# Two cross-attention layers in one kernel: layer 1's scores are computed once and kept in SBUF, and the row of maxima is added by VectorE and GpSimd

## The chip, the cores and the metric

The kernel runs on one core of one Trainium2 chip. The metric is the device time of one execution in microseconds (us); lower is better. Before the change the median of three runs is 3543.13 us (3540.61 to 3550.69). The engines are called PE (TensorE), DVE (VectorE), ACT (ScalarE), POOL (GpSimd) and SP (the queue that issues nearly all DMAs).

## The reference

Two layers of cross-attention follow each other, for 4 batches of 512 queries (320 channels, 20 heads of 16) over one context of 1024 tokens (512 channels), all in float32. In both layers the tokens fall into text and image ("ip") tokens with a softmax of their own. Cut to what matters:

```python
# layer 0: text = first 1020 tokens, ip = last 4
scores_t = einsum('bhsd,bhtd->bhst', q, k_t) * attn_scale
probs_t = softmax(scores_t)
text_out = einsum('bhst,bhtd->bhsd', probs_t, v_t)
attn_scores = einsum('bhsd,bhnd->bhsn', q, k_ip) * attn_scale
qsem = l2norm(einsum('bhst,bte->bhse', probs_t, text_ehs))
fused = attn_scores + 0.5 * einsum('bhse,bne->bhsn', qsem, l2norm(ip_ehs))
ip_out = einsum('bhsn,bhnd->bhsd', softmax(fused) * spatial_mask, v_ip)
x = (text_out + ip_out) @ W_out + b_out + x

# layer 1: text = first 77 tokens, ip = the other 947
out_text = attend(q, k, v, sm_scale)        # softmax over 77 tokens
out_ip = attend(q, k_ip, v_ip, sm_scale)    # softmax over 947 tokens
out = (out_text + out_ip) @ Wo.T + bo + x
```

Layer 1's queries come from layer 0's output; keys and values of both layers come from the context alone.

## The kernel before

A *turn* is 128 queries of one batch; there are 16 turns. A *group* is four heads of layer 0 in one turn, so there are 80 groups, and the main loop runs over them. Each group has two units (two heads each), each unit four parts (`part0` to `part3`, pieces of layer 0's large product of probabilities with values and context, tiles `b`), and after each part there is a *stop*, numbered k = 0 to 7 over the group. The function `stop` (L1054) puts other work between the parts:

- `item()`: one entry of a queue: the transposes of layer 1's maxima (`sub`), a turn's finishing steps (`late`), or a step of the next batch's projections (`proj`);
- at k = 0 and 1 `fill0`: one half (512 tokens) of layer 0's scores of the next group, `sc`, by 32 products in four row groups of PE; ACT copies them to SBUF (`e`), DVE reduces their maxima over the tokens that lie on one partition (`m`). The two score tiles are read by ACT and DVE in turn, and a tile's buffer is free when both are done;
- at k = 2 `max0`: PE transposes `m`, DVE reduces to one row (`zz`), transposes it (`zt`); SP writes it to DRAM (`zd`) and broadcasts it to all partitions (`bc`, 256 KB);
- at k = 4, 5, 5, 6 an entry of `ew` (end of `end_stop`): DVE adds the row to a quarter of the scores, ACT takes the exponential, POOL subtracts one half from the other for two of four;
- at k = 2, 4, 5, 6 `l1_step`: a step of layer 1, four to every four heads.

Layer 1 computes its scores twice. `do_max` multiplies queries by keys (`mx`, two products of 512 columns) with queries on the partitions and DVE reduces them from PSUM; `do_sub` transposes the negative maxima and adds them as extra rows to the queries (`qa`), next to rows of ones in `kq[1]` that choose between the text's maximum and the ip's. `do_exp` multiplies again (`ex`, 19 rows, two heads at a time) with tokens on the partitions, so that the maximum is already subtracted, and ACT takes the exponential straight from PSUM. `do_pv` multiplies by the values (`pv`), and `normalise` and `project` end the turn. After the last group the last turn's layer 1 runs alone (the tail).

PE, DVE and SP's broadcasts keep the order of the program text (`keep_in_program_order`); the other instructions are placed on their engine by the framework when the program is built, and each engine runs its own in that fixed order. The DVE operations of helper `vec` carry line 87, PE products 77, PE transposes 92.

A unit's parts depend on each other: `part2` adds products to a tile that DVE first has to copy (`p`, in `part1`), and `part3` adds to a tile that DVE first has to read (`c`, at the end of `part2`).

Of the kernel before, what the change touches and what calls it, by code (L numbers as in the profile page):

```python
# [20 lines left out]
P = 128  # L21
# [3 lines left out]
NIP = 4  # L25
# [30 lines left out]
def xattn_pair(ctx_stack: ExitStack, tc: tile.TileContext, a: dict, out: bass.AP):  # L56
# [9 lines left out]
    e1p = pool("e1p", 6)  # L66
# [61 lines left out]
    kq = [[cst.tile([P, T], F32, name=f"kq{l}_{i}") for i in range(1 + l)] for l in range(2)]  # L128
    qq = [[cst.tile([P, P], F32, name=f"qq{l}_{i}") for i in range(1 + l)] for l in range(2)]
    nmz = [cst.tile([P, P], F32, name=f"nmz_{i}") for i in range(2)]  # L130
    zz = cst.tile([P, ZW], F32, name="zz")
# [4 lines left out]
    own = cst.tile([H * NIP, H, D], F32, name="own")  # L136
# [59 lines left out]
    nc.vector.memset(zz, 0.0)  # L196
    nc.gpsimd.memset(wo1, 0.0)

    for i in range(2):
        nc.vector.memset(qq[1][i], 0.0)  # L200
        nc.vector.memset(nmz[i], 0.0)
# [7 lines left out]
    nc.gpsimd.tensor_copy(kq[1][1], kq[1][0])  # L209
# [7 lines left out]
    for n in ("21", "t4"):  # L217
# [10 lines left out]
                            pattern=[[-NIP, H], [0, D]], channel_multiplier=1)  # L228
    nc.gpsimd.affine_select(out=own, in_=own, compare_op=ALU.is_ge, fill=0.0, base=NIP - 1,
                            pattern=[[NIP, H], [0, D]], channel_multiplier=-1)  # L230
# [4 lines left out]
    def normalised_ip():  # L235
        ipraw = st2.tile([B * NIP, E], F32, tag="pc", name="ipraw")
        for b in range(B):
            nc.scalar.dma_start(ipraw[b * NIP : (b + 1) * NIP, :], a["ctx_2048"][b, NTXT0:T, :])
        ipsq = st2.tile([B * NIP, E], F32, tag="pc", name="ipsq")
# [63 lines left out]
    def queries(t, ns, w, dst, name, tag):  # L303

        n = ns * P
        o = st2.tile([P, NC, n], F32, tag=tag, name=f"qs_{name}")
# [18 lines left out]
    def projections(b):  # L325
# [11 lines left out]
        def quarter(n):  # L337
# [108 lines left out]
            def values_ip():  # L446

                w = load_w(b, "L0_xattn_W_v_ip")
                z.vip = st2.tile([H * NIP, C], F32, tag="vip", name=f"vip_{b}")
                rep = big.tile([P, EC, H, NIP], F32, tag="xin", name=f"iprep_{b}")  # L450
                nc.gpsimd.tensor_copy(rep, box["cT"][:, :, QT - NIP : QT].unsqueeze(2).to_broadcast([P, EC, H, NIP]))
                pt = tp(f"pt_vip_{b}")
                for e in range(EC):
                    mm(pt[: H * NIP, 0:C], rep[:, e].rearrange("p h n -> p (h n)"), w[:, e, 0:C], e == 0, e == EC - 1)
                vec.tensor_tensor(z.vip, pt[: H * NIP, 0:C], own.rearrange("p h d -> p (h d)"), ALU.mult)
# [33 lines left out]
    hold = [0]  # L489
    ready = {}  # L490
# [4 lines left out]
    def load_quad(l, z, turn, g):  # L495
# [3 lines left out]
        k = buffer(l, turn, g)  # L499
# [5 lines left out]
    def buffer(l, turn, g):  # L505
        return (turn * HG + g) % 2 if l else 0

    def fill(c, m, name):


        ps = [ps_sc.tile([P, 2, 512], F32, tag="sc", name=f"sc{name}_{c}_{i}") for i in range(2)]
        for j in range(TH):
            t = (TH * c + j) * P
            for r in range(4):
                mm(ps[r // 2][:, r % 2, j * P : (j + 1) * P], kq[0][0][32 * r : 32 * r + D, t : t + P],
                   qq[0][0][32 * r : 32 * r + D, :], True, True)
        e = [ep.tile([P, 2, TH, P], F32, tag="e0", name=f"e{name}_{c}_{i}") for i in range(2)]

        for i in range(2):
# [3 lines left out]
                              ps[j][:, :, 0 : (TH - c) * P].rearrange("p h (t s) -> p h s t", s=P), AX.X, ALU.max)  # L523
        return e

    def layer1(turn):

        b, s = TURNS[turn]  # L530
        z = zs[b]
        e1, ms, qas, vq, box = {}, {}, {}, {}, {}

        def name_of(g):
            return f"1_{turn}_{g}"

        def do_max(g, i, half):

            if g not in ms:
                ms[g] = st2.tile([P, 2, 4], F32, tag="m1", name=f"m{name_of(g)}")  # L540
            k, m = buffer(1, turn, g), ms[g][:, :, 2 * i : 2 * i + 2]
            if tail[0]:
                ps = [tail_bank(f"mx{name_of(g)}_{i}_{half}_{j}").unsqueeze(1) for j in range(2)]
            else:
                ps = [ps_sc.tile([P, 2, 512], F32, tag="sc", name=f"mx{name_of(g)}_{i}_{half}")]
            for j in range(2):
                r = 32 * (2 * i + j)
                o = ps[j][:, 0, :] if tail[0] else ps[0][:, j, :]
                mm(o, qq[1][k][r : r + D, :], kq[1][k][r : r + D, half * 512 : half * 512 + 512], True, True)

            def rows(row):
                return nmz[k].rearrange("p (r n) -> p r n", r=4)[:, 2 * i : 2 * i + 2, row]

            n = 2 // len(ps)
            for j, p in enumerate(ps):
                mine = slice(j * n, j * n + n)
                if half == 0:
                    vec.tensor_reduce(rows(R_TXT)[:, mine], p[:, :, 0:NTXT1], AX.X, ALU.max, negate=True)
                vec.tensor_reduce(m[:, half, mine], p[:, :, 0 if half else NTXT1 : 512], AX.X, ALU.max, negate=True)
            if half:  # L560
                vec.tensor_tensor(rows(R_IP), m[:, 0, :], m[:, 1, :], ALU.min)

        def do_sub(g):

            k = buffer(1, turn, g)
            pt = (tail_bank if tail[0] else tp)(f"pt_nm{name_of(g)}")
            tr(pt[:, 0:P], nmz[k], ident)
            qas[g] = st2.tile([P, P], F32, tag="qa", name=f"qa{name_of(g)}")
            vec.tensor_tensor(qas[g], pt[:, 0:P], qq[1][k], ALU.add)

        def do_exp(g, i, half):

            k, name = buffer(1, turn, g), f"{name_of(g)}_{i}_{half}"
            ps = ps_sc.tile([P, 2, 512], F32, tag="sc", name=f"ex{name}")
            for j in range(TH):
                t = (TH * half + j) * P
                for h in range(2):
                    r = 32 * (2 * i + h)
                    mm(ps[:, h, j * P : (j + 1) * P], kq[1][k][r : r + KR, t : t + P], qas[g][r : r + KR, :], True, True)
            e = e1p.tile([P, 2, TH, P], F32, tag="e1", name=f"e{name}")  # L580
            nc.scalar.activation(e.rearrange("p i j s -> p (i j s)"), ps.rearrange("p i n -> p (i n)"), AF.Exp)  # L581
            e1[g, i, half] = e

        def do_pv(g):

            v, name = vq.pop(g), name_of(g)
            e = [[e1.pop((g, i, half)) for i in range(2)] for half in range(2)]
            pv = tp(f"pv{name}")
            for r in range(4):
                mm(pv[32 * r : 32 * r + 32, P : 2 * P], v[:, 0, r * V1W : r * V1W + 32], e[0][r // 2][:, r % 2, 0, :],  # L590
                   True, True)
            for t in range(TT):
                for r in range(4):
                    mm(pv[32 * r : 32 * r + 32, 0:P], v[:, t + 1, r * V1W : r * V1W + 32],
                       e[t // TH][r // 2][:, r % 2, t % TH, :], t == 0, t == TT - 1)
            pc = st2.tile([P, 2 * P], F32, tag="pc", name=f"pc{name}")
            nc.scalar.copy(pc, pv[:, 0 : 2 * P])
            late.append(lambda: normalise(g, pc))

        def normalise(g, pc):  # L600
            if "o" not in box:
                box["o"] = big.tile([P, HG, P], F32, tag="o1", name=f"o1_{turn}")
            name = name_of(g)
            d = big.tile([P, 2 * P], F32, tag="den", name=f"den{name}")
# [25 lines left out]
        def values(g):  # L630
            if g < HG:
                vq[g] = st2.tile([P, TT + 1, V1Q], F32, tag="v1q", name=f"v1q_{turn}_{g}")
                nc.sync.dma_start(vq[g], z.v1d[:, :, g * 4 * V1W : g * 4 * V1W + V1Q])

        def load(g):
            load_quad(1, z, turn, g)

        def first_maxima(half):
            x = (turn * HG) % 2
            if half == 0:  # L640
                load(1)
                values(0)
            do_max(0, x, half)
            do_max(0, 1 - x, half)
# [3 lines left out]
        def step(g, k):  # L648


            x, half = (k + turn * HG + g) % 2, k // 2

            def after(n):

                return (me, g + n) if g + n < HG else (ready[turn + 1], g + n - HG) if turn + 1 in ready else None

            nxt = after(1)

            def maxima():
                if nxt and (g + 1 < HG or nxt[0].linked):  # L660
                    nxt[0].do_max(nxt[1], 1 - x, half)

            if tail[0]:

                if k == 0:
                    maxima()
                    if pend:
                        pend.pop()()
                if sub:
                    sub.popleft()()  # L670
                do_exp(g, x, half)
                if k:
                    maxima()
            else:
                maxima()
                if sub:
                    sub.popleft()()
                do_exp(g, x, half)
                if k == 0 and pend:
                    pend.pop()()  # L680
            if k == 1 and nxt and (g + 1 < HG or nxt[0].linked):
                nxt[0].values(nxt[1])
            if k == 3:
                pend.append(lambda: do_pv(g))
                if nxt and (g + 1 < HG or nxt[0].linked):
                    sub.append(lambda: nxt[0].do_sub(nxt[1]))
                two = after(2)
# [445 lines left out]
```

## Time and profile before

| | before |
|---|---|
| median of three runs | 3543.13 us |
| span of the profiled execution | 3537.1 us |
| first group to last group's start | 91.5 to 3364.2 us |
| `b` products on `xv_t`, mean of one record | 400 ns, 2560 records |
| ACT exponential of layer 1 from PSUM, 128x1024 | 1018 ns, 320 times |
| ACT copy of layer 0's scores, 128x1024 | 1012 ns, 320 times |
| DVE reduce of scores 128x1024 / 128x768 | 1220 / 957 ns, 160 times each |
| DVE add of the row, 128x1024 / 128x768 | 1227 / 995 ns, 160 times each |
| POOL operation on 128x512 with two SBUF inputs | 1269 to 1309 ns |
| broadcast `bc`, 256 KB | 80 times |

The page gives for each engine its busy time and share of the span, then slices of the span in tenths, then the chain of work that ended last. In a timeline a line is: start, time, engine, line, operation, tile written <- tiles read, shapes, count, and in brackets the idle time before it and what ended it. A product of PE appears as two records, and the ends of PE's records are modelled, so neighbours overlap: the time that a piece takes is read from its start to the next piece's start.

### The profile page before, as it was taken

The page shows a single profiled execution, that of the slowest core. Times are in us where ns is not written, and L with a number is a line of the kernel's source. Part 1 is how long each engine was busy: PE and PEld are TensorE (multiplying, and loading weights), DVE is VectorE, ACT ScalarE, POOL GpSimd, SP SyncE. Part 2 cuts the span into 40 slices and gives each one's busy share as a digit, 9 for nine tenths or more (in the row PEclk, how much of TensorE's full clock was granted, in tenths as well). Part 3 has the DMA queues.
Part 4 walks back from the last instruction along what each step waited for, and adds up shares of the span by engine and source line. Part 5 has one row for each costly group of instructions (what it writes and reads, how often), then busy time and mean ns, then how long its engine had stood idle before and what let it go on. Part 6 is the DMA issues. An engine that isn't in the chain of part 4 may idle for free.

```text
span 3537.1 us, 74110 instructions
## 1 busy us (share of the span) xinstructions
PE 3458.4 (98%) x29060; PEld 2757.2 (78%) x29060; DVE 2057.4 (58%) x3814; ACT 1477.9 (42%) x2807; POOL 993.7 (28%) x1050
## 2 busy tenths in 40 slices
PE   7999999999999999999999999999999999999989
PEld 6777777777787878777778888877778877777866
DVE  2344556666655655566665554656666666666644
ACT  1333344444434444444444443444444444444422
POOL 2322222332222222233222222222332332232310
PEclk9999999999999999999999999999999999999976
DMA  7454332222344244222234434322232222222211
GB/s 218 102 136 118 90 73 41 49 41 51 90 99 106 61 107 102 51 60 44 49 88 116 101 79 99 69 57 47 47 88 48 51 43 52 47 47 45 48 29 35
DMA packets 700570, 258.76 MB, mean 73 GB/s; under 512 B 567952, under 2 KB 673904, under 8 KB 700224
## 3 DMA queue, kind: packets, MB, share of 16 engines
q1 hardware_dynamic: 699184, 250.42, 31.5%
q8 instruction: 232, 3.80, 0.5%
q0 software_dynamic: 864, 3.41, 0.4%
q14 instruction: 114, 0.93, 0.1%
q10 hardware_dynamic: 176, 0.20, 0.0%
HBM read 213.51 MB, written 40.33 MB: 72 GB/s over the span
## 4 chain that ended last, share of the span: by engine, by line
PE 83%; DVE 9%; DMA 3%; issue 2%; SPq 2%; ACT 1%; POOL 0%; DVEq 0%; POOLq 0%; ACTq 0%
PE b L77 51%; PE ex L77 5%; PE sc L77 4%; PE pv L77 4%; PE pt_v L77 4%; PE mx L77 4%; PE pt_k L77 4%; DVE m L87 2%; PE pt_y L77 2%; DVE e L87 2%; PE pt_q L77 2%; DMA bc<-zd 2%; PE mx L92 1%; DVE den L87 1%; DVE n L87 1%
## 5 line engine op out<-in xcount | busy, mean ns | idle before, releaser
L77 PE MATMUL b<-xv_t,e 128*128 128x277 f32 x2560 | 659.6, 400 | 10.5 <-DVE c L87 9.9
L77 PE MATMUL b<-xv,e 128*128 128x277 f32 (+1 forms) x2560 | 651.2, 407 | 2.8 <-ACT e L778 2.8
L77 PEld LDWEIGHTS b<-xv,e 128*128 128x128 f32 x2560 | 479.7, 190 | 136.4 <-ACT e L778 3.3
L77 PEld LDWEIGHTS b<-xv_t,e 128*128 128x128 f32 x2560 | 473.0, 190 | 117.4 <-DVE c L87 15.9
L778 ACT ACTIVATE e<-e 128x1024 f32<-128x1024 f32 x320 | 338.2, 1057 | 407.6 <-DVE e L87 401.7
L873 POOL TENSOR_TENSOR e<-e,s 128x512 f32<-128x512 f32 x160 | 203.1, 1269 | 1028.0 <-PE b L77 1027.9
L87 DVE TENSOR_REDUCE m<-sc 128x256 f32<-128x1024 f32 (+1 forms) x320 | 341.6, 1089 | 160.9 <-PE sc L77 154.3
L87 DVE TENSOR_REDUCE m<-mx 128x2 f32<-128x870 f32 (+3 forms) x345 | 366.6, 1066 | 97.6 <-PE ex L77 74.3
L581 ACT ACTIVATE e<-ex 128x1024 f32<-128x1024 f32 x320 | 325.3, 1018 | 194.5 <-PE ex L77 194.2
L520 ACT COPY e<-sc 128x1024 f32<-128x1024 f32 x320 | 322.8, 1012 | 175.0 <-PE sc L77 131.6
L858 ACT ACTIVATE junk<-c 128x256 f32<-128x256 f32 x480 | 198.9, 414 | 460.5 <-DVE c L87 455.3
L87 DVE TENSOR_TENSOR e<-e,bc 128x1024 f32<-128x1024 f32 x320 | 355.2, 1111 | 59.4 <-DMA bc<-zd 59.1
L87 DVE TENSOR_TENSOR c<-b,p 128x256 f32<-128x256 f32 x320 | 133.6, 417 | 427.8 <-PE b L77 419.6
L77 PE MATMUL ex<-qa,kq 19*128 19x128 f32 x5120 | 377.0, 288 | 4.3 <-DVE qa L87 3.1
L77 PE MATMUL mx<-kq,qq 16*128 16x512 f32 x1280 | 375.8, 662 | 5.2 <-DMA qq<-q1d 2.9
L854 POOL TENSOR_TENSOR s<-e,e 128x512 f32<-128x512 f32 x160 | 203.6, 1273 | 472.6 <-ACT e L778 303.4
L77 PEld LDWEIGHTS ex<-qa,kq 19*128 19x128 f32 x5120 | 318.4, 191 | 16.8 <-issue 5.8
L77 PE MATMUL b<-xs,e 128*128 128x256 f32 x1280 | 319.7, 393 | 3.8 <-DVE p L87 3.3
L77 PE MATMUL b<-xs_t,e 128*128 128x256 f32 x1280 | 318.4, 392 | 1.3 <-POOL e L873 1.3
L780 POOL TENSOR_TENSOR e<-e 128x512 f32<-128x512 f32 x160 | 209.4, 1309 | 380.8 <-ACT e L778 380.8
L77 PE MATMUL b<-xs_t,s 128*128 128x256 f32 x1280 | 303.0, 379 | 0.4
L77 PEld LDWEIGHTS b<-xs_t,e 128*128 128x128 f32 x1280 | 230.4, 189 | 51.5 <-issue 13.7
(190 smaller groups left out, 4140.1 us busy)
## 6 DMA issues: line engine op xcount, KB each, us to landing
kq<-kd SPq DMA_DIRECT2D x640, 64.0 KB
v1q<-v1d SPq DMA_DIRECT2D x80, 373.5 KB
bc<-zd SPq DMA_DIRECT2D x80, 256.0 KB
xv<-v0d SPq DMA_DIRECT2D x480, 42.0 KB
xv_t<-v0d SPq DMA_DIRECT2D x320, 42.0 KB
L_xattn_W_k<-in_L_xattn_W_k_dram SPq DMA_DIRECT2D x13, 640.0 KB
L_xattn_Wv_ip<-in_L_xattn_Wv_ip_dram SPq DMA_DIRECT2D x13, 640.0 KB
raw<-in_ctx_dram SPq DMA_DIRECT2D x32, 256.0 KB
```

The source lines that it names most:

```text
L77: tc.keep_in_program_order(nc.tensor.matmul(out, lhsT=lhsT, rhs=rhs, start=start, stop=stop, skip_group_check=on))
L87: return lambda *args, **kw: keep(getattr(self.engine, name)(*args, **kw))
L92: tc.keep_in_program_order(nc.tensor.transpose(out, in_, ident))
L520: nc.scalar.copy(e[i].rearrange("p h t s -> p (h t s)"), ps[i].rearrange("p h n -> p (h n)"))
L581: nc.scalar.activation(e.rearrange("p i j s -> p (i j s)"), ps.rearrange("p i n -> p (i n)"), AF.Exp)
L778: nc.scalar.activation(flat, flat, AF.Exp)
L780: nc.gpsimd.tensor_tensor(e[:, 1], e[:, 1], e[:, 0], ALU.subtract)
L854: nc.gpsimd.tensor_tensor(self.s2, self.e("21"), self.e("22"), ALU.add)
L858: nc.scalar.activation(junk, x, AF.Square, accum_out=self.w["ss"][:, self.h + r, k : k + 1])
L873: nc.gpsimd.tensor_tensor(self.e("11"), self.e("11"), self.s2, ALU.add)
```

## The change

For all turns but the last, layer 1's scores are computed once, with tokens on the partitions, by the same `fill` as layer 0's: 32 products a half, ACT copies to SBUF, DVE reduces and a maximum of the halves. `Once.maxima` transposes the first block of 128 tokens and the maxima of the rest (eight transposes), DVE makes two rows (text and ip), which go by DRAM to all partitions in three broadcasts (512 KB in all). `Once.do_exp` adds the row: for the first half of the tokens on DVE, with the first 128-token block apart, for the second half on POOL; ACT takes the exponential from SBUF. `once(k)` replaces `l1_step` in `stop`: half fills at k = 3 and 4, maxima at k = 7, adds and exponentials at k = 2, 3, 6, 7 of the next group, `pv` at k = 1 after that. The last turn keeps the old way (`twice`) in the tail; there must be no layer-1 work left when it starts.

The buffer of keys for layer 1 is now single, the pool of `e` tiles for layer 1 has 8 buffers instead of 6, and tiles are moved between pools. Layer 0's scores of the four ip tokens are no longer kept from the transposes (`ips`): `load_ip_scores` loads queries and keys again and `exps` multiplies them in three products a turn. `values_ip` masks with two selections on POOL instead of a product with `own`.

```diff
-    e1p = pool("e1p", 6)
+    e1p = pool("e1p", 8)
...
-    kq = [[cst.tile([P, T], F32, name=f"kq{l}_{i}") for i in range(1 + l)] for l in range(2)]
+    kq = [[cst.tile([P, T], F32, name=f"kq{l}")] for l in range(2)]
...
-    def fill(c, m, name):
+    def fill(l, c, m, pl, tag, name):
...
+        lo, hi = (1 - c, TH) if l else (0, TH - c)
         for i in range(2):
             nc.scalar.copy(e[i].rearrange("p h t s -> p (h t s)"), ps[i].rearrange("p h n -> p (h n)"))
             j = 1 - i
             vec.tensor_reduce(m[:, c, 2 * j : 2 * j + 2, :],
-                              ps[j][:, :, 0 : (TH - c) * P].rearrange("p h (t s) -> p h s t", s=P), AX.X, ALU.max)
+                              ps[j][:, :, lo * P : hi * P].rearrange("p h (t s) -> p h s t", s=P), AX.X, ALU.max)
+        if c:
+            vec.tensor_tensor(m[:, 0], m[:, 0], m[:, 1], ALU.max)
         return e
...
+    class Once:
+
+        def __init__(self, turn, g, z, done, pl=None, tag="e1"):
+            self.turn, self.g, self.z, self.done, self.name = turn, g, z, done, f"1_{turn}_{g}"
+            self.pl, self.tag, self.e = pl or e1p, tag, {}
+            self.work = deque(lambda c=c, i=i: self.do_exp(c, i) for c in range(2) for i in range(2))
+
+        def fill(self, c):
+            if c == 0:
+                self.m = big.tile([P, 2, 4, P], F32, tag="m0", name=f"m{self.name}")
+            self.e[c] = fill(1, c, self.m, self.pl, self.tag, self.name)
+            if c:
+                loaded.clear()
+                load_next()
+
+        def maxima(self):
+
+            ps = ps_sc.tile([P, 2, 512], F32, tag="sc", name=f"mx{self.name}")
+            rest, first = [ps[:, k, :].rearrange("p (h t) -> p h t", h=4) for k in range(2)]
+            for h in range(4):
+                tr(first[:, h, :], self.e[0][h // 2][:, h % 2, 0, :], ident)
+            for h in range(4):
+                tr(rest[:, h, :], self.m[:, 0, h, :], ident)
+            z = zz[1]
+            vec.tensor_reduce(z[:, 0:4], first[:, :, 0:NTXT1], AX.X, ALU.max, negate=True)
+            vec.tensor_reduce(z[:, 8:12], first[:, :, NTXT1:], AX.X, ALU.max, negate=True)
+            vec.tensor_reduce(z[:, 4:8], rest, AX.X, ALU.max, negate=True)
+            vec.tensor_tensor(z[:, 4:8], z[:, 4:8], z[:, 8:12], ALU.min)
+            zt = st2.tile([P, ZW], F32, tag="zt", name=f"zt{self.name}")
+            vec.transpose(zt, z)
+            zd = spread(zt, 8, "zd1", self.name)
+            self.bc = bc = big.tile([P, 2, 4, P], F32, tag="bc1", name=f"bc{self.name}")
+            keep(nc.sync.dma_start(bc[:NTXT1, 0], zd[0:4, :].partition_broadcast(NTXT1)))
+            keep(nc.sync.dma_start(bc[NTXT1:, 0], zd[4:8, :].partition_broadcast(P - NTXT1)))
+            keep(nc.sync.dma_start(bc[:, 1], zd[4:8, :].partition_broadcast(P)))
+            self.v = load_values(self.z, self.turn, self.g)
+
+        def do_exp(self, c, i):
+            e, (first, rest) = self.e[c][i], [self.bc[:, k, 2 * i : 2 * i + 2, :] for k in range(2)]
+            if c == 0:
+                vec.tensor_tensor(e[:, :, 0, :], e[:, :, 0, :], first, ALU.add)
+            x = e[:, :, 1 - c :, :]
+            (nc.gpsimd if c else vec).tensor_tensor(x, x, rest.unsqueeze(2).to_broadcast([P, 2, TH - 1 + c, P]), ALU.add)
+            flat = e.rearrange("p h t s -> p (h t s)")
+            nc.scalar.activation(flat, flat, AF.Exp)
+
+        def values(self):
+            add_values(self.name, self.v, self.e, lambda pc: self.done(self.g, pc))
...
+    def load_next():
+        if waiting and not loaded:
+            turn, g, z, done = waiting[0]
+            load_quad(1, z, turn, g)
+            loaded.append(stops[0])
+
+    def take(*where):
+        if not loaded or stops[0] < loaded[0] + 2:
+            return None
+        o = Once(*waiting.popleft(), *where)
+        inside.append(o)
+        return o
...
         def exps():
+            pt = tp(f"pt_s_{name}")
+            for c, (c0, n) in enumerate(CK):
+                mm(pt[:, 0 : H * NIP], qf[:n, c, :], kip[:n, c].rearrange("p h n -> p (h n)"), c == 0, c == NC - 1)
             vec.tensor_tensor(sem, sem, wide(rn), ALU.mult)
-            vec.scalar_tensor_tensor(pe, sem, SEM_SCALE, ips, ALU.mult, ALU.add)
+            vec.scalar_tensor_tensor(pe, sem, SEM_SCALE, pt[:, 0 : H * NIP].rearrange("p (h n) -> p h n", h=H),
+                                     ALU.mult, ALU.add)
...
-        if k in (2, 4, 5) or k == 6 and gi < len(G) - 2 or ending[0] and k < 2:
-            l1_step()
         if k == 2:
             max0(gi + 1)
+        once(k)
         end_stop(k)
+
+    def once(k):
+
+        if k in ((0, 3) if ending[0] else (3,)):
+            filling[0] = take(*((ep, "e0") if ending[0] and k == 0 else ()))
+        o = filling[0]
+        if o and k in (0, 3):
+            o.fill(0)
+        if o and k in (1, 4):
+            o.fill(1)
+        if o and k in ((2, 7) if ending[0] else (7,)):
+            o.maxima()
+            o.ready = stops[0] + 3
+            filling[0] = None
+        if inside:
+            first = inside[0]
+            if not first.work and k == 1:
+                inside.popleft().values()
+            elif first is not filling[0] and k in (2, 3, 6, 7) and first.work and stops[0] >= first.ready:
+                first.work.popleft()()
```

## The prediction

> **What bounds the kernel now.** I read the page first (engine totals, clock, chain), then TensorE's waits, then the timeline of one group, then single waits. A group is one pass of the main loop: four heads of layer 0, eight stops k = 0 to 7, 80 groups in all.
>
> ```profile
> PE 3458.4 (98%) x29060; PEld 2757.2 (78%) x29060; DVE 2057.4 (58%) x3814; ACT 1477.9 (42%) x2807; POOL 993.7 (28%) x1050
> PEclk9999999999999999999999999999999999999976
> PE 83%; DVE 9%; DMA 3%; issue 2%; SPq 2%; ACT 1%; POOL 0%; DVEq 0%; POOLq 0%; ACTq 0%
> ```
>
> TensorE (PE) is busy in nearly every slice at its full clock until the tail (the last two digits); the other engines have room. The list of waits gives PE 9.9 us on VectorE's `c` and 3.3 us on its `p` in the whole span. So a group costs its PE work: the timeline has one without extra items from 3174.94 to 3210.96, 36.0 us. What a layer-1 piece costs must be read from starts, not from the groups' busy times, because two products overlap:
>
> ```profile
> 3178.91 1.17 PE L77 MATMUL sc<-qq,kq 16*128 16x128 f32 x32
> 3180.01 0.48 PE L77 MATMUL b<-xs_t,e 128*128 128x256 f32 x1
> ...
> 3202.99 0.70 PE L77 MATMUL mx<-kq,qq 16*128 16x512 f32 x2
> 3203.01 0.71 PE L77 MATMUL ex<-qa,kq 19*128 19x128 f32 x8
> 3203.53 0.59 PE L77 MATMUL mx<-kq,qq 16*128 16x512 f32 x2
> 3203.55 0.61 PE L77 MATMUL ex<-qa,kq 19*128 19x128 f32 x8
> 3204.10 0.48 PE L77 MATMUL b<-xs,e 128*128 128x256 f32 x1
> ```
>
> Both kinds of scores run side by side: one layer-1 step takes 3204.10 - 3202.99 = 1.1 us, although `mx` and `ex` show some 376 us of busy time each. Half a fill of layer 0 (`sc`) takes the same 1.1 us.
>
> **PE work.** Per four heads of layer 1 the change removes four steps (4.4) and the transpose of `nmz` (0.1). It adds two half fills (2.2) and eight transposes; four of them take 3190.16 - 3189.66 = 0.5, so 1.0. That is 1.3 us less in each of the 75 groups that carry layer 1: -97. New products for the IP scores, nine-product `pt_q` being 2.0 us: 3/9 of it, 0.65 x 16 = +10. Net -87.
>
> **What goes to the others.** VectorE loses per four heads the reduces on `mx` (2 x 1.22 + 2 x 1.05 + 2 x 0.31 + 2 x 0.22 = 5.6) and `qa` 0.3; it gains reduces 2 x 0.96 + 2 x 1.22, the maximum 0.69, three reduces on transposes, `zz`'s minimum and transpose (together 1.95), and adds 2 x (0.34 + 0.97): 9.6. ScalarE gains four copies of 1.01, GpSimd two adds. SP gains seven issues of 0.33 and 512 KB of broadcast; it and the DMA queues (31.5% busy) have room, and the single layer-1 `kq` is reloaded at k = 4 for k = 3 of the next group, over 20 us of cover for eight issues. Initial memsets, `own` and the dropped `ips` copy lie beside PE. The totals fit (VectorE some 28 of 35 us a group), but order matters: the built program's order on each engine is fixed, and three places make PE wait.
>
> **First wait: a broadcast, two GpSimd adds and ScalarE's queue.** On ScalarE the two exponentials fed by GpSimd stand, in nearly every group, ahead of the copies of layer 0's second half fill (k = 1). Behind those copies stand VectorE's second reduce, its maximum and both `drop` maxima; behind these PE's transposes at k = 2 and VectorE's two `c`, which PE's last product of the unit waits for. Let 0 be the start of the group's first product, the transposes of the row of maxima ending there (they are at k = 7). The row goes the same way as layer 0's:
>
> ```profile
> 3191.77 0.21 DVE L87 STREAM_TRANSPOSE zt<-zz 128x32 f32<-128x32 f32 x1
> 3192.01 1.25 SPq L765 DMA_DIRECT2D zd<-zt  x4
> 3195.22 0.34 SPq L767 DMA_DIRECT2D bc<-zd  x1
> 3198.93 1.23 DVE L87 TENSOR_TENSOR e<-e,bc 128x1024 f32<-128x1024 f32 x1 [0.30 <-DMA bc<-zd]
> ```
>
> VectorE ends `zt` at 1.5 (reduces of 308 and 204 elements run under the second four transposes, then 512 elements 0.69, minimum 0.2, transpose 0.2). Four `zd` issues: 2.8. In SP's order three `xv` windows follow, the last released by the product that ends at 4.0: 4.6. Three `bc` issues of 0.34: 5.65. Landing 3.4 after the issue's end (row above): 9.1. One GpSimd add of 1024 elements: the 512-element row takes 1.27 and the 256-element row 0.73, so 2.35. Adds end at 11.5 and 13.8; second exponential (1.06) at 15.0; copies at 16.0 and 17.0; reduce 17.0, maximum 17.7, two `drop` maxima 18.7; PE transposes at 18.8. PE itself is there after 4.0 + 1.1 + 3.65 + 1.1 + 2.1 (`pv`) + 3.8 = 15.75. With the two `c` (2 x 0.42) its next product starts at 19.65, not 16.25: **3.4 us**. If `bc` is issued as `zd` lands and all land together, 8.6 and 2.8 us; if 512 KB in three parts take turns, 10.7 and 5.0 us. I take 3.4, as the row's 256 KB are the nearest. Cover comes only from items at k = 0 to 2. Read from the starts of the groups in the timeline, some 21 of the 75 hold the next batch's projections (43 to 50 us each, the others 36.0 to 40.7) and are covered, since each of their stops brings PE work of its own; the query product (2.0) and small items (0.5) help in 11 groups each: 54 x 3.4 - 27 = **+157**.
>
> **Second and third wait: emptied stops.** The old steps at k = 5 and 6 stood between dependent products. After the second layer-1 fill (k = 4) VectorE has two reduces 2.44, maximum 0.69, layer 0's add 1.23, copy `p` 0.42 = 4.8, PE only 3.65 before it needs `p`: 1.0 to 1.6, taken as 1.4. At k = 6 PE waits for `c`; where no step stood there, before shows it:
>
> ```profile
> 3397.54 0.42 DVE L87 TENSOR_TENSOR c<-b,p 128x256 f32<-128x256 f32 x1 [1.37 <-PE b L77]
> ...
> 3398.02 2.13 PE L77 MATMUL b<-xv_t,e 128*128 128x277 f32 x8 [0.52 <-DVE c L87]
> ```
>
> 0.52 to 0.65. `multiply` and the next transposes cover both in 11 groups: 43 x (1.4 + 0.65) = **+88**.
>
> **The port.** GpSimd can hold up VectorE or be held up:
>
> ```profile
> 625.39 1.22 DVE L87 TENSOR_TENSOR e<-e,bc 128x1024 f32<-128x1024 f32 x1
> ...
> 625.37 2.38 POOL L780 TENSOR_TENSOR e<-e 128x512 f32<-128x512 f32 x1 [6.60 <-ACT e L778]
> ```
>
> GpSimd's 1.27 became 2.38, longer by VectorE's add. In the new window VectorE mostly reads PSUM; closer packed adds at k = 5 may collide: 0 to 1.3 a group, taken 0.5 x 54 = **+27**. The Trainium skill ("SBUF — State Buffer", Who interferes with whom) says a VectorE operation with two SBUF inputs and a GpSimd operation that reads SBUF exclude each other for the whole instruction, against handing adds to GpSimd; if that hit both new adds once a group by 1.2 us, the first wait would grow by up to 2.4.
>
> **The clock.** After a wait of 2.32 us by TensorE:
>
> ```profile
> 3402.70:3406.10 3.40, 1.16 (x6) 0.40 (x10) 2.70 (x9) 0.76 (x3) 0.00 (x0) 1.00 0.08 18
> 3406.10:3409.50 3.40, 3.40 (x68) 3.40 (x71) 1.84 (x7) 0.00 (x0) 0.00 (x0) 0.50 0.00 0
> ```
>
> the second stretch (the column after POOL is the granted clock) ran at 0.50, losing 1.7 us of work. At 3.4 us a wait this can come in most uncovered groups, partly under the second wait: 0 to +90, taken **+25**. The Trainium skill ("TensorE: Matmul & The Clock Gate", Part 1) puts the gate at a whole idle window of about 3.4 us; by that a 3.4 us wait would almost never close it and the term would be 0; the row closes it after 2.32.
>
> **The tail** keeps its old form; two `pv` replace steps beside the same late chain: -5 to +10, taken +5.
>
> Sum: -87 + 157 + 88 + 27 + 25 + 5 = +215 on the profiled 3537.1, 3752; the runs' median lies 6.0 above that span, so **3758**.
>
> **Rivals.**
> - *The rows hide the new waits* (faster). Only PE work changes: 3543 - 87 = 3456. It decides if `bc` lands so early that both adds and exponentials end before PE's half fill at 9.85, a landing near 3. For it: PE is 98% busy, all others under 60%. Against it: the `zd` and `bc` way alone takes 7 us above.
> - *Only the emptied stops cost*: -87 + 88, about 3544, the same, if the first wait is swallowed.
> - *Port and VectorE bind*: every GpSimd add blocks a two-input VectorE operation, 28 + 12 us, groups of over 42: 3543 + 54 x 6 = 3867 and above.
> - *The gate stays at half* as in the tail (the last slices' 7 and 6), groups far longer, 4000 or more.
>
> **How the numbers follow.** Forecast 0.70, its own range 3640 to 3890 (wait 2.8 to 5.0, clock 0 to 90, port 0 to 70); hidden 0.10; same 0.05; port 0.11; gate 0.04. 0.3%, 11 us, is what a measurement can tell. Faster 0.10, same 0.05, slower 0.85. The range 3530 to 3900 takes in the forecast's own and the case of no change; it leaves out the hidden case, the gate and the upper half of the port, some 0.19.
>
> **What would show it.** After: groups of about 40 to 42 us where they were 36.0; PE busy well under 98%; waits of PE's `mx` on `m` and of `b` on `p` and `c`; ScalarE idle on GpSimd's `e`; slices with PEclk under 9. If PE is still near 98% and ScalarE's wait for GpSimd ends before the copies, the prediction is wrong.

## The result, and the profile after

The changed kernel takes 4057.26 us (median of 4 runs, 4046.72 to 4069.05) beside 3546.91 us for the kernel before: 1.143 times as long, 95% interval 1.1398 to 1.1463. The forecast was 3758, with a range up to 3900. So the direction was right and the size too small by more than half: 215 us more were forecast, 510 came.

The page of the profile after, its lines that answer to those shown of before (engine totals, granted clock, chain by engine):

```profile
PE 3556.2 (88%) x28481; PEld 2773.4 (68%) x28481; DVE 2517.8 (62%) x4101; ACT 1758.1 (43%) x3107; POOL 1502.7 (37%) x1242
PEclk9999999999999999999999999989999999999986
PE 52%; DVE 15%; DMA 11%; POOL 8%; ACT 6%; issue 3%; SPq 3%; DVEq 0%; POOLq 0%; ACTq 0%
```

TensorE went from 98% to 88% busy, and its share of the chain from 83% to 52%: more of the time now goes the way from TensorE through the other engines and back. The profiled span grew by 525.0 us (3537.1 to 4062.1). TensorE's idle time grew by 427.2 (from 3537.1 - 3458.4 = 78.7 to 505.9), and its busy time grew too, by 97.8, although it has 579 instructions fewer. The clock digits are nines, which hides the second fact: a digit averages over some 100 us.

The waits of TensorE in the profile after (us in total, number, longest):

```profile
PE b L77 <- ACT u L935: 131.7, 54, 5.5
PE mx L92 <- DVE m L87: 87.6, 45, 3.2
PE b L77 <- DVE p L87: 87.2, 45, 3.4
PE b L77 <- DVE c L87: 45.6, 84, 1.1
PE pt_p L92 <- ACT pc L545: 29.1, 15, 4.6
PE mx L92 <- DVE pT L87: 23.9, 15, 2.0
```

One group in the timeline after, from TensorE's first product at 3550.78 (start, duration, engine, operation; in brackets the idle time before it and its releaser):

```profile
3550.78 4.04 PE L77 MATMUL b<-xv,e 128*128 128x298 f32 x16
...
3551.76 0.18 DVE L87 COPY pv<-b 128x21 f32<-128x21 f32 x1 [1.49 <-ACT junk L907]
3551.86 1.34 DVE L87 TENSOR_REDUCE zz<-mx 128x4 f32<-128x308 f32 x3
...
3553.03 1.27 POOL L922 TENSOR_TENSOR e<-e,s 128x512 f32<-128x512 f32 x1 [0.27 <-PE b L77]
3553.24 1.08 DVE L87 TENSOR_TENSOR zz<-zz 128x4 f32<-128x4 f32 x1
3554.36 0.21 DVE L87 STREAM_TRANSPOSE zt<-zz 128x32 f32<-128x32 f32 x1
...
3558.38 0.35 SPq L587 DMA_DIRECT2D bc<-zd  x1
...
3563.78 4.65 POOL L595 TENSOR_TENSOR e<-e,bc 128x1024 f32<-128x1024 f32 x2 [7.60 <-DMA bc<-zd]
...
3566.16 1.06 ACT L597 ACTIVATE e<-e 128x1024 f32<-128x1024 f32 x1 [7.87 <-POOL e L595]
3567.12 0.35 ACT L935 COPY u<-b 128x256 f32<-128x256 f32 x1
3567.53 2.13 PE L77 MATMUL b<-xv_t,e 128*128 128x277 f32 x8 [2.82 <-ACT u L935]
3568.47 1.06 ACT L597 ACTIVATE e<-e 128x1024 f32<-128x1024 f32 x1 [0.99 <-POOL e L595]
3569.43 1.91 ACT L519 COPY e<-sc 128x1024 f32<-128x1024 f32 x2
...
3572.81 1.09 PE L92 MATMUL mx<-ident,m 128*128 128x128 f32 x4 [3.15 <-DVE m L87]
```

Read it as one queue. ScalarE stands still for 7.87 us until GpSimd's first add ends; behind the exponential stands the copy `u`, which TensorE waits for (2.82); behind the second exponential stand layer 0's copies, behind these VectorE's maxima, and TensorE waits a second time (3.15). The four transposes then take 1.09 us; four took 0.5 before. The windows of the same stretch say why (stretch, busy us of PE, PEld, VectorE, ScalarE, GpSimd, then the granted clock, DMA share, GB/s):

```profile
3569.40:3572.80 3.40, 0.26 (x2) 0.02 (x1) 2.27 (x4) 2.21 (x4) 0.00 (x0) 0.99 0.49 96
3572.80:3576.20 3.40, 3.39 (x10) 2.51 (x11) 3.37 (x7) 1.02 (x4) 0.19 (x1) 0.51 0.12 29
```

After a stretch with 0.26 us of TensorE's work the next one runs at half clock. Such stretches come to 496.2 us in the profiled span after and to 117.4 in that of before. Before, most of that lies in the tail (95.5 us); after, 77 stretches lie in the main loop, 372 us in all, each one to three times 3.4 us long. At half clock half of the time is lost.

### The profile page after: what moved, and what is told of

Its sections match the earlier page's. It is cut to its first block, busy times and chain, and to the rows that moved or that the text cites. A ratio compares the mean times of both kernels' runs of the same rounds, so it can differ in the third digit from the quotient of the medians.

```text
span 4062.1 us, 74077 instructions
## 1 busy us (share of the span) xinstructions
PE 3556.2 (88%) x28481; PEld 2773.4 (68%) x28481; DVE 2517.8 (62%) x4101; ACT 1758.1 (43%) x3107; POOL 1502.7 (37%) x1242
## 4 chain that ended last, share of the span: by engine, by line
PE 52%; DVE 15%; DMA 11%; POOL 8%; ACT 6%; issue 3%; SPq 3%; DVEq 0%; POOLq 0%; ACTq 0%
PE b L77 32%; DMA bc<-zd 8%; POOL e L595 8%; DVE m L87 6%; DVE e L87 5%; PE sc L77 5%; PE pt_v L77 3%; ACT e L597 3%; PE pt_k L77 3%; PE mx L92 2%; ACT e L519 2%; PE pt_q L77 2%; PE pt_y L77 2%; PE pv L77 2%; DVE c L87 1%
## 5 line engine op out<-in xcount | busy, mean ns | idle before, releaser
L87 DVE TENSOR_REDUCE m<-sc 128x256 f32<-128x1024 f32 (+1 forms) x620 | 664.4, 1088 | 723.2 <-ACT e L519 440.1
L77 PE MATMUL b<-xv_t,e 128*128 128x277 f32 x2560 | 772.6, 451 | 178.5 <-ACT u L935 131.7
L519 ACT COPY e<-sc 128x1024 f32<-128x1024 f32 x620 | 610.9, 1010 | 169.6 <-PE sc L77 118.4
L87 DVE TENSOR_TENSOR e<-e,bc 128x1024 f32<-128x1024 f32 (+1 forms) x620 | 672.9, 1105 | 0.8 <-issue 0.4
L597 ACT ACTIVATE e<-e 128x1024 f32<-128x1024 f32 x300 | 316.8, 1056 | 690.7 <-POOL e L595 538.5
L595 POOL TENSOR_TENSOR e<-e,bc 128x1024 f32<-128x1024 f32 x150 | 351.3, 2362 | 482.4 <-DMA bc<-zd 482.4
L827 ACT ACTIVATE e<-e 128x1024 f32<-128x1024 f32 x320 | 338.3, 1057 | 343.1 <-DVE e L87 340.7
L77 PE MATMUL b<-xs,e 128*128 128x256 f32 x1280 | 326.5, 399 | 87.2 <-DVE p L87 87.2
L77 PEld LDWEIGHTS sc<-qq,kq 16*128 16x128 f32 x9920 | 313.4, 189 | 127.3 <-issue 107.1
L77 PE MATMUL sc<-qq,kq 16*128 16x128 f32 x9920 | 374.0, 286 | 13.5 <-ACT e L519 10.2
L829 POOL TENSOR_TENSOR e<-e 128x512 f32<-128x512 f32 x160 | 249.4, 1559 | 313.9 <-ACT e L827 309.2
L77 PEld LDWEIGHTS b<-xs,e 128*128 128x128 f32 x1280 | 240.6, 196 | 152.4 <-issue 119.2
L77 PEld LDWEIGHTS b<-xs_t,s 128*128 128x128 f32 x1280 | 243.8, 190 | 33.4
```

The costliest lines, as they stand in the source:

```text
L77: tc.keep_in_program_order(nc.tensor.matmul(out, lhsT=lhsT, rhs=rhs, start=start, stop=stop, skip_group_check=on))
L87: return lambda *args, **kw: keep(getattr(self.engine, name)(*args, **kw))
L519: nc.scalar.copy(e[i].rearrange("p h t s -> p (h t s)"), ps[i].rearrange("p h n -> p (h n)"))
L595: (nc.gpsimd if c else vec).tensor_tensor(x, x, rest.unsqueeze(2).to_broadcast([P, 2, TH - 1 + c, P]), ALU.add)
L597: nc.scalar.activation(flat, flat, AF.Exp)
L827: nc.scalar.activation(flat, flat, AF.Exp)
```

## The experiments

All times are medians; each ratio is to the kernel before, run on the same chip in the same job. e1, e2, e10 and e11 are edits of the changed kernel, e3 to e8 of e1, e9 and e12 of e7. The last two columns come from the profiled run of each; that of e4 took 3753.5 us and that of e7 3543.4, so they lie off the medians. Half clock is the time in the profiled span in which the granted clock was 0.5.

| run | us | ratio (95%) | PE busy us | half clock us |
|---|---|---|---|---|
| changed kernel | 4057.3 | 1.1430 (1.1398 to 1.1463) | 3556.2 | 496.2 |
| e1 exponentials in order | 3719.6 | 1.0487 (1.0455 to 1.0519) | 3432.2 | 226.4 |
| e2 adds on VectorE | 3689.0 | 1.0402 (1.0377 to 1.0427) | 3418.0 | 183.3 |
| e3 layer 0's adds later | 3670.1 | 1.0341 (1.0311 to 1.0370) | 3418.6 | 182.1 |
| e4 fill at k = 5 | 3733.3 | 1.0534 (1.0499 to 1.0569) | 3457.2 | 292.2 |
| e5 `p` on ScalarE | 3624.6 | 1.0209 (1.0182 to 1.0236) | 3391.0 | 151.2 |
| e6 maxima at k = 6 | 3660.6 | 1.0320 (1.0296 to 1.0344) | 3422.9 | 243.6 |
| e7 = e5 and e6 | 3556.3 | 1.0026 (1.0008 to 1.0044) | 3370.7 | 104.5 |
| e8 = e7, adds on VectorE | 3638.1 | 1.0255 (1.0233 to 1.0277) | 3434.3 | 230.1 |
| e9 = e7, three small waits | 3530.8 | 0.9953 (0.9938 to 0.9969) | 3381.9 | 122.9 |
| e10 changed kernel with filler | 4178.6 | 1.1780 (1.1762 to 1.1798) | 3952.8 | 186.0 |
| e11 needed row first | 3987.6 | 1.1237 (1.1217 to 1.1258) | 3536.1 | 431.5 |
| e12 `p` ahead of a copy | 3554.0 | 1.0021 (1.0006 to 1.0037) | 3402.8 | 182.3 |

**e1: only ScalarE's order.** The edit pins the two exponentials behind what ScalarE was given before them; nothing else is edited.

```diff
-            nc.scalar.activation(flat, flat, AF.Exp)
+            x = nc.scalar.activation(flat, flat, AF.Exp)
+            if c:
+                keep(x)
```

> Only the two exponentials of layer 1's second half (fed by GpSimd's adds) are pinned behind what ScalarE was given before them, so that on ScalarE they stand behind layer 0's copies at k = 1 instead of ahead of u and of these copies. Nothing is removed: the same 150 GpSimd adds, the same broadcast. Theory A (ScalarE's order is the first wait): TensorE's waits on u (131.7 us) and of mx on m (87.6) go nearly to nothing, and with them most of the half-clock stretches (TensorE's busy 3556 falls towards 3371 + 60): 4057 - 219 - 120 = about 3720, between 3640 and 3800. Theory B (the broadcast and GpSimd are late whatever the order, and TensorE then waits elsewhere for the same row): under 80 us gained, over 3975. Theory C (the gate, not the waits, is what costs: TensorE stays at half clock once per group for the waits on p and c that are left): waits go but busy stays at about 3550, 3830 to 3900.

Measured: 3719.6, as theory A put it. ScalarE in one group of e1's timeline: `u` and both copies run when their inputs are there, and the exponentials come at the end.

```profile
3271.01 0.37 ACT L937 COPY u<-b 128x256 f32<-128x256 f32 x1 [1.32 <-PE b L77]
3272.19 2.09 ACT L519 COPY e<-sc 128x1024 f32<-128x1024 f32 x2 [0.81 <-PE sc L77]
...
3283.34 1.06 ACT L597 ACTIVATE e<-e 128x1024 f32<-128x1024 f32 x1 [1.71 <-DVE e L87]
```

And TensorE's waits in e1:

```profile
PE b L77 <- DVE p L87: 122.0, 45, 3.4
PE b L77 <- DVE c L87: 49.6, 102, 1.1
PE mx L92 <- DVE pT L87: 18.9, 15, 2.8
PE mx L92 <- DVE m L87: 18.7, 18, 2.6
```

The wait on `u` fell from 131.7 to 0.2, on `m` from 87.6 to 18.7, on `pc` from 29.1 to 0.5, and waits of `pv` on ScalarE's evacuations (19.8) went: 249 us less idle. Busy time fell by 124 with the same instructions, and the wait on `p` rose by 35, since TensorE now comes to it earlier: 249 + 124 - 35 = 338 of the 346 us by which the span fell. Theories B and C fall. The broadcast, GpSimd's adds and their lateness are still there (the first add starts 11.8 us after the group's first product, 12.3 in the changed kernel; medians of groups 8 to 78), yet TensorE's waits on `u`, `m`, `pc` and of `pv` come to 19.4 us in place of 268. Two thirds of the loss was the place of two exponentials in one queue.

**e2: the second half's adds on VectorE.**

```diff
-            (nc.gpsimd if c else vec).tensor_tensor(x, x, rest..., ALU.add)
+            vec.tensor_tensor(x, x, rest..., ALU.add)
```

> Layer 1's second-half adds go to VectorE instead of GpSimd; as VectorE runs in program order, the exponentials behind them also come at k = 6 and 7, as in e1. Theory A: the first wait goes as in e1, and VectorE gets 150 x 1.22 = 183 us more, 2.4 of some 40 us a group, at k = 6 and 7 where c follows: e1's time plus 0 to 60. Theory D (sharing a port with GpSimd is what slows VectorE: the minimum of 128x4 took 1.08 us beside a GpSimd operation): VectorE's other rows get shorter (reduces, minimum) by more than it gains, GpSimd's rows go back to 1270 to 1310 ns, and this is faster than e1 by 20 us or more. Theory B: no gain over the changed kernel beyond 80 us.

Measured: 3689.0, 31 faster than e1, but not for theory D's reason. GpSimd's remaining operations did not get shorter: the subtraction of 128x512 elements at 1554 ns, 1475 in e1, 1309 before the change. VectorE's adds of 1024 elements stayed long too: 1573 ns, 1533 in e1, 1227 before. So the adds given to GpSimd are not what makes these rows longer; what is left is that VectorE's own adds meet GpSimd's old operations more often, which no run tried by itself. What went is e1's wait on `m` (18.7, none in e2), half of that on `pT`, and some half clock. Where the other waits are gone too, e8 shows the opposite sign, so this edit's worth depends on its surroundings.

**e3 and e4: the wait on `p`.** e3 moves layer 0's adds by one stop, e4 layer 1's second half fill.

```diff
-        for _ in range({4: 1, 5: 2, 6: 1}.get(k, 0)):
+        for _ in range({5: 2, 6: 1, 7: 1}.get(k, 0)):
```

> e1, with layer 0's four adds and exponentials one stop later (5, 5, 6, 7 instead of 4, 5, 5, 6). Theory A2 (the second wait, b on p, 87.2 us, is VectorE's queue at k = 4: two reduces, a maximum and one add of 1.2 us ahead of p): p comes 1.2 us earlier, its wait falls to 45 x 0.7 = 30, 50 us or more faster than e1. Rival: the add taken from ahead of p stands ahead of c instead, and the wait moves there: within 20 us of e1, c's wait up by what p's went down.

```diff
-        if o and k in (1, 4):
+        if o and k in ((1, 5) if not ending[0] else (1, 4)):
```

> e1, with layer 1's second half fill at k = 5 instead of k = 4, so that TensorE has 1.1 us of it in an emptied stop and VectorE has two reduces and a maximum fewer ahead of p. Theory A2: p's wait goes to under 10 us, c's wait at k = 6 may grow by the reduces (3.1 us of VectorE behind p, 3.65 us of TensorE beside it): 40 to 90 us faster than e1. Rival: the reduces ahead of c make a wait as long as p's was, time within 20 us of e1.

e3 gained 49 us: `p` fell from 122.0 to 73.9, less than expected, and `c` did not rise, as the rival said, but fell from 49.6 to 40.7. e4's median was 14 us above e1's, with runs that overlap (3728.8 to 3753.5, 3709.5 to 3732.8): its two waits only changed places, as its rival said.

```profile
PE b L77 <- DVE c L87: 176.8, 118, 3.1
...
PE b L77 <- DVE p L87: 2.3, 1, 2.3
```

VectorE keeps its order here; moving the reduces from ahead of `p` to ahead of `c` moved the wait with them.

**e5 and e6: `p` on ScalarE; the row's transposes in the emptied stop.**

```diff
-            vec.tensor_copy(self.p5, self.b3)
+            if self.i:
+                nc.scalar.copy(self.p5, self.b3)
+            else:
+                vec.tensor_copy(self.p5, self.b3)
```

> e1 (3719.6 us), with the copy p of the unit's second half (k = 5) made by ScalarE instead of VectorE; its operands are the same. Theory A2 (p is late because of what stands ahead of it on VectorE: two reduces, a maximum and an add): the product behind p then waits only for a ScalarE copy of 0.4 us; e1's wait on p, 122.0 us, falls to about 45 x 0.5 = 22, and some half-clock time with it: 3719.6 - 100 - 20 = 3600, between 3570 and 3630. Rival (VectorE itself is full at k = 4 to 6, so that the wait only moves to the next VectorE result, c, as it did when the fill was moved to k = 5: p 122 to 2, c 50 to 177): within 30 us of e1, c's wait up by 80 or more.

```diff
-        if o and k in ((2, 7) if ending[0] else (7,)):
+        if o and k in ((2, 7) if ending[0] else (6,)):
             o.maxima()
-            o.ready = stops[0] + 3
+            o.ready = stops[0] + (3 if ending[0] else 4)
```

> e1, with the eight transposes of the row of maxima at k = 6 instead of k = 7, so that TensorE has 1.0 us of work in the emptied stop and the row starts about 4 us earlier. Theory A3 (the third wait, b on c, is the lack of any TensorE work at k = 6): c's wait of 49.6 falls to about 10, 3680 +- 15. Rival (VectorE gets five small operations ahead of layer 0's adds, and the row that lands earlier changes nothing else): c falls but p and m rise by as much, within 15 of e1.

e5 gained 95 us: the wait on `p` went from 122.0 to 29.0, now on ScalarE, `c` rose by 18 and `m` by 18. e6 gained 59, a little more than forecast: `c` went from 49.6 to 8.2, and `m` from 18.7 to 0.8 with the row that starts a stop earlier; the wait of `pt_q` on ScalarE's `xT` rose from 2.9 to 17.7. The line of each, e5's first:

```profile
PE b L77 <- ACT p L935: 29.0, 26, 1.1
...
PE b L77 <- DVE c L87: 8.2, 34, 0.5
```

Both mechanisms hold: each edit took away most of the wait that it was made for.

**e7 and e8: both together, and with the adds on VectorE.**

> e5 and e6 together: all three waits named in the prediction are then answered. If the three waits and the clock that they cost are all of the loss, what is left is TensorE's work, 87 us less than in the kernel before: 3460 to 3560, faster than before if under 3537. If port and VectorE bind (VectorE at 71% of e1's span with GpSimd beside it), 3600 or above with waits on m or c still.

> e7 with the second-half adds on VectorE (the half of the change that was given to GpSimd taken back). If the port is what GpSimd's adds cost: 20 to 40 us faster than e7, as e2 was 30 faster than e1. If VectorE becomes the bound (2.4 us more of about 37 a group): slower than e7 by 20 or more, with TensorE waiting on c and m.

e7's page and waits:

```profile
PE 3370.7 (95%) x28481; PEld 2684.8 (76%) x28481; DVE 2535.9 (72%) x4021; ACT 1779.2 (50%) x3187; POOL 1463.3 (41%) x1242
```

```profile
PE b L77 <- ACT p L935: 34.5, 31, 1.1
PE mx L92 <- DVE pT L87: 21.0, 15, 1.8
PE b L77 <- DVE c L87: 17.6, 71, 1.0
PE pt_q L77 <- ACT xT L119: 16.9, 11, 2.5
```

e7 is 501 us faster than the changed kernel with the same work on TensorE, and 0.26% (0.08 to 0.44) above the kernel before; it lies at the upper end of what was expected. TensorE's busy time is 3370.7: the 87 us of saved work, which the first trace hid, are there. e8 is 82 us slower than e7: with 150 more adds on VectorE, `pt_q` waits 37.6 us on ScalarE's and 12.8 on VectorE's `xT`, the half fills (`sc`) 29.2 on ScalarE's copies, and half clock doubles; `c` and `m`, which were expected to be the waits, were not. Once the order is right, the half on GpSimd is worth having.

**e9: three small waits of e7's profile** (the core of the edit; four of the eight transposes at k = 5, another PSUM tile for `pt_p`, layer 1's transposed rows copied by VectorE alone).

```diff
+        if o and k in ((2, 7) if ending[0] else (5,)):
+            o.first_maxima()
...
-            pt = tp(f"pt_p_{name}")
+            pt = ps_sc.tile([P, 2, 512], F32, tag="sc", name=f"pt_p_{name}")[:, 0, :]
...
+            move = vec.tensor_copy if ns == 1 else evac
```

> e7 (3556.3 us) with three small waits of its profile answered: four of the eight transposes of the row of maxima at k = 5 and four at k = 6 (for p's wait of 34.5 us), another PSUM tile for the transpose behind which max0's transposes waited on pT (21.0), and the two copies of layer 1's transposed rows on VectorE (pt_q waited 16.9 on ScalarE's xT and 4.0 on VectorE's). If waits are all that is left above TensorE's 3371 us of work: 15 + 18 + 15 less, about 3508, faster than the kernel before by 1% (3490 to 3530). If VectorE or the port is the bound: 3550 or more, with the waits moved to c and m.

Measured: 3530.8, a ratio of 0.9953 (0.9938 to 0.9969): the change's idea, with the order and the engines of some copies chosen to suit it, beats the kernel before by 0.5%. It lies just above what was expected: the split took `p` off (4.4 us), but a wait of the transposes on a copy came in its place.

```profile
PE b L77 <- DVE c L87: 27.2, 64, 1.0
PE mx L92 <- ACT e L520: 22.4, 30, 0.8
PE pt_q L77 <- DVE xT L87: 15.3, 16, 2.2
```

None of these edits was tried on the kernel before. The waits that they answer are small in it: 3.3 us on `p`, 2.7 on `pT`, 3.9 on `xT`.

**e10: filler in the waits.** The filler's products start sums of their own in banks where sums of layer 0 are open, and what this kernel returns is not the reference's result; it serves for its times alone.

```diff
+        def filler(self, bank, n):
+            if 7 <= self.gi < len(G) - 1:
+                for _ in range(n):
+                    mm(bank[:, 3 * P : 4 * P], ident, ident, True, True, True)
```

> The changed kernel, with TensorE products of the identity with itself written to columns of a bank that nothing reads, where TensorE waits: 16 ahead of the wait for u, 10 ahead of the wait for m, 8 ahead of the wait for p, in groups 7 to 78 (about 0.12 us each, 4.1 us a group, 294 us in all); they wait for nothing themselves. The chain that the waits are for is unchanged. Theory C1 (the clock closes on TensorE's idleness in these waits and costs 185 us): the half-clock stretches go, mean clock above 0.97, and the time falls to 3900 to 3990, although TensorE does more. Theory C2 (the clock falls for another reason, or what is lost at half clock is hidden in the next wait): 4050 or more, up to 4200 where groups have no wait to fill.

The time, 4178.6, lies in theory C2's range, but for a reason that neither gave. A filler product took 0.223 us (16 in 3732.14 - 3728.57), not 0.12, so 72 groups x 34 x 0.223 = 546 us of it were added. The clock part held: half clock fell from 496.2 to 186.0 us, and the mean granted clock rose from 0.939 to 0.978. The stretches around the first wait in e10:

```profile
3728.00:3731.40 3.40, 3.40 (x30) 3.32 (x29) 0.00 (x0) 1.32 (x2) 3.40 (x2) 1.00 0.24 67
3731.40:3734.80 3.40, 3.40 (x25) 3.04 (x24) 1.15 (x2) 3.15 (x4) 0.19 (x1) 1.00 0.47 111
3734.80:3738.20 3.40, 3.31 (x24) 2.86 (x23) 3.33 (x8) 1.02 (x4) 0.00 (x0) 1.00 0.13 17
```

Waits on `u`, `m` and `p` fell by 240 together, those on `pc` and `pT` by 40, and TensorE's busy time without the filler (3952.8 - 546 = 3407) by 149; 546 - 240 - 40 - 149 = 117, and the span grew by 113. So the half clock follows from idleness in these waits, and the 149 us that TensorE got back did not turn up again as waits elsewhere: its lost time lay on the path.

**e11: the broadcast that GpSimd reads, issued first of three.**

```diff
+            keep(nc.sync.dma_start(bc[:, 1], zd[4:8, :].partition_broadcast(P)))
             keep(nc.sync.dma_start(bc[:NTXT1, 0], zd[0:4, :].partition_broadcast(NTXT1)))
             keep(nc.sync.dma_start(bc[NTXT1:, 0], zd[4:8, :].partition_broadcast(P - NTXT1)))
-            keep(nc.sync.dma_start(bc[:, 1], zd[4:8, :].partition_broadcast(P)))
```

> The changed kernel, with the broadcast that GpSimd's adds read (the 128 partitions of the rows without the first 77 tokens) issued first of the three instead of last. The prediction let all three land 3.4 us after the last one's issue; one group of the profile after shows 5.05 us. If the three parts take turns on the queues, this one lands 0.7 us earlier for its issue and some 1 us for the bytes of the other two (154 KB of 512 in all are before it), and the first wait shortens by 1 to 2 us in some 54 groups: 50 to 130 us faster than 4057. If the landing is bound by its own bytes or by zd: only the two issues, 0.7 x 54 = 38 or less.

Measured: 3987.6, 70 us faster, inside the first theory's range. One group of e11:

```profile
3470.15 0.34 SPq L585 DMA_DIRECT2D bc<-zd  x1
...
3473.89 4.65 POOL L595 TENSOR_TENSOR e<-e,bc 128x1024 f32<-128x1024 f32 x2 [5.02 <-DMA bc<-zd]
```

GpSimd starts 3.40 us after the end of the first issue; in the changed kernel it started 5.05 after the end of the third (3558.73 to 3563.78). Over groups 8 to 78 its adds start 2.4 us earlier in the group (median 9.9, was 12.3). The median time from the end of the needed issue to the first add fell by 1.1 us (4.4 to 3.3); `zt` also ended earlier (3.8 to 2.0), with a minimum that met GpSimd less often, and what each is worth in the total is not separated. The queue on ScalarE still costs: `u` and `m` fell by 66 us each, but the half fills' wait on ScalarE's copies rose from 10.2 to 79.0 and that on `p` from 87.2 to 122.2.

**e12: `p` ahead of a copy.** e7's eight transposes at k = 6, e9's other two edits, layer 1's last copy pinned behind `p`, and one of layer 0's adds moved from k = 5 to k = 6.

```diff
                 nc.scalar.copy(self.p5, self.b3)
+                while behind_p:
+                    keep(behind_p.pop()())
```

> e9 (3530.8 us) without its split (all eight transposes again at k = 6, as in e7), with ScalarE's second copy of layer 1's second half fill pinned behind p, and layer 0's adds at k = 4, 5, 6, 6 instead of 4, 5, 5, 6, so that c has 1.2 us less of VectorE ahead of it. e9's plain groups still idle for 0.75 (transposes on a ScalarE copy) and 0.58 us (c). If these were all that is left: 30 groups x 1.3 = 40 less, 3490 (3475 to 3510), faster than the kernel before by 1.5%. If layer 0's exponentials, now later on ScalarE, hold up the next group's p or first copies instead: 3520 to 3560, with new waits on p or m.

A miss: 3554.0, 23 slower than e9. `p` and `c` did go (6.0 and 8.1 us), and plain groups took 35.5 us by their starts, where e9's took 36.5. But `pt_q` now waits for VectorE's copy of `xT`, and more was lost there; the add that was moved later stands ahead of that copy, which is the likely cause and was not tried alone:

```profile
PE pt_q L77 <- DVE xT L87: 49.1, 16, 4.6
```

## Why the prediction was right and wrong

**PE work, -87: right.** 3458.4 - 87 = 3371; e7's busy time is 3370.7 and e9's 3381.9. That e7 agrees to 0.3 us is luck, since busy time takes in what is lost at half clock, and that differs by some us (104.5 us of half clock in e7, 122.9 in e9, 117.4 before). The tail, +5: right in size; from the start of the last group's second unit to the end it took 153.3 us before and 158.5 after.

**First wait, +157: right mechanism, too small.** e1 shows that it is ScalarE's queue. The waits that e1 removes or cuts came to 268 us in the profile after (`u` 131.7, `m` 87.6, `pc` 29.1, `pv` 19.8), 111 more than forecast and more than the range's upper wait gives (54 x 5.0 - 27 = 243). The chain was right in its steps, and each step was later than put:

| from the group's first product, us | predicted | median, groups 8 to 78 |
|---|---|---|
| VectorE ends `zt` | 1.5 | 3.8 |
| four `zd` issued | 2.8 | 5.1 |
| last `bc` issued | 5.65 | 7.95 |
| row landed, first add starts | 9.1 | 12.3 |
| second add ends | 13.8 | 17.0 |

Three things were mis-sized and one was left out. "VectorE ends `zt` at 1.5" let the reduces run under the transposes; a copy of the unit before stands ahead of them on VectorE and waits for ScalarE's square, so they began at 1.08. The minimum of 128x4, put at 0.2, took 1.08 while GpSimd held the port (0.16 in other groups). The landing was taken from one broadcast, 3.4; with three the median was 4.4 (5.05 in the group shown, which is the upper bound given: 10.7 - 5.65). A GpSimd add itself took 2.36, as put. And the copy `u` was overlooked: it stands behind the first exponential, so TensorE stops one product earlier, and then again for `m`.

**The 21 groups with projections, which "are covered": wrong.** A turn of five groups with projections took 230 us before and 255 to 260 after, about 5.5 us a group. Their stops bring work for TensorE, but also evacuations for the same ScalarE queue (`pv` on `xT`, `cT` and `kst` are in the list of waits). In e1 these turns took 232 to 245 us.

**Second and third wait, +88: right mechanism, a little small.** `p` cost 84 us more than before (put at 60) and `c` 36 (put at 28); e5 and e6 each took most of theirs away. With the first wait gone they were larger, 122.0 and 49.6.

**Port, +27: not settled.** Rows grew (VectorE's add of 1024 elements from 1227 to 1535 ns, GpSimd's subtraction from 1309 to 1559), and they were as long in e2, where VectorE does the new adds. In e7, with the new adds on GpSimd, VectorE's add took 1234 ns again, though GpSimd's subtraction took 1621. So the rows depend on what meets what in the built order. What share lay on the path was not isolated.

**Clock, +25: the step that failed.** "At 3.4 us a wait this can come in most uncovered groups, partly under the second wait: 0 to +90, taken +25." It came about once in every group, and cost 3556.2 - 3370.7 = 185 us, twice the upper bound; half of the half-clock time that was added gives the same, (496.2 - 117.4) / 2 = 189. Of the 299 us by which the forecast fell short, 160 are this term, and 111 the first wait. The prediction had the row that shows it (half clock after 2.32 us of idleness) and then took a quarter of its bound. It also treated one wait per group where there were two with 2.1 us of work between them. The Trainium skill ("TensorE: Matmul & The Clock Gate", Part 1) speaks of a whole idle window of about 3.4 us; here no wait of the shown group reached that (2.82 and 3.15), and the clock still fell. The measurement decides.

Together: -87 + 268 + 84 + 36 + 185 + 21 (`pT`) = 507 of the 525 us. Of the rivals, the one in which rows hide the waits (3456) was not reached even by e9; port and VectorE did not bind, since plain groups took 36.6 us in e7, under the 42 that it needed (its own sum, 28 + 12, makes 40). The measured time lies where the gate that stays at half was put, 4000 or more, but not for that reason: the clock came back after each stretch, and half clock was 372 of some 3800 us of the main loop.

## What to carry to other kernels

When work moves to an engine that was idle, read the built order of the engine behind it: an early place in a queue is a loss if its input comes late, and pinning two instructions was worth 338 us here. A wait of TensorE cost its length here and, where it brought the clock down, about half of the 3.4 us after it as well; size both, and count each wait of a group. Moving VectorE's work past one deadline can just move the wait to the next one (e4; in e3 both fell); giving it to another engine took most of the wait away (e5).

## What the runs showed of the hardware

- Two waits of 2.82 and 3.15 us with 2.1 us of work between them brought the granted clock to 0.51 for 3.4 us; products that nothing reads kept it at 1.00 (e10).
- A 128x4 minimum on VectorE took 1.08 us beside a GpSimd add of 1.27 us and 0.16 without one. The Trainium skill ("SBUF — State Buffer", Who interferes with whom) has this as an exclusive port pair; the small operation pays the large one's remaining time.
- Three broadcasts issued in a row (154 and 102 KB, then 256 KB): the last was usable 5.05 us after its issue ended (median of groups 8 to 78: 4.4); the same one issued first, 3.40 (median 3.3).
